# Reordering the start of an attention and mixture-of-experts kernel: later loads, q by pairs, v first

## The chip, the cores and the metric

The kernel runs on one core of a Trainium2 chip. The metric is the time of one execution in microseconds (us); lower is better. TensorE (PE) multiplies, VectorE (DVE), ScalarE (ACT) and GpSimd (POOL) do the rest, and every data transfer of this kernel is issued from one queue, that of SyncE (SP).

## The reference

The input x is 8 batches of 512 tokens of 256 numbers. Per batch (layernorm over the last axis, no scale or offset):

```
n  = layernorm(x)
q, k, v = split(n @ w_in.T + b_in)                  # 16 heads of 16
att = softmax(einsum('blhd,bmhd->blmh', q, k) / 4, axis=2)
opt = einsum('blmh,blhd->blhd', att, v)             # row sums of att, times v
x1 = x + layernorm(opt @ w_out.T + b_out)
f  = layernorm(x1)
e  = argmax(f @ gate_W.T + gate_b)                  # one of 8 experts
h  = relu(f @ wi_W.T + wi_b + (f @ lora_A[e].T) @ lora_B[e].T)
out = x1 + layernorm(h @ wo_W.T + wo_b)
```

The attention weights are summed, not multiplied with v, so what the kernel needs of each head is the maximum and the sum of the exponentials of each score row, 128 rows by 512 at a time. All is in float32. To keep precision, factors of the dense products are split into a high part and a low part (names that end in h and l), and a product is made of three.

## The kernel before, in words

**Tiling.** A batch is two *units* of 256 tokens, a unit two *chunks* of 128. The 16 heads make eight *pairs*, and pairs 0 to 3 come from the first half of the heads (group 0), 4 to 7 from the second (group 1). Per batch:

- `prepare`: x is normalised (`st_x`, `mv_x`, `nr_x`, `ln_x`, with the batch's number behind), transposed on TensorE (`pst_xn`) and split into `xnh` and `xnl` (lines 521 and 528).
- `project`: for each group, TensorE makes q and then k in `psqk` (line 486, six products of 512 columns each). For batch 0, ScalarE writes the high part and VectorE the low part of a tile `hl_0_group_t`, t being 0 for q and 1 for k (lines 362 and 375). Later batches go through `full_qk` on ScalarE and then GpSimd.
- `lay_out_k` (line 572): two transfers from SP copy a pair's k into `rows_batch_pair`. `lay_out_q`: for the first unit of batch 0 two transfers per pair (line 593) into one of three buffers, `q_0_pair`; for every other unit four transfers per pair and unit (line 606) into one of six constant tiles q0 to q5, in which the other head's half is zero.
- `scores`: a product per head and chunk (`sc`, line 642, all 128 rows; in the first unit of batch 0 two products of 64 rows, line 651), the row maximum on VectorE (`nmax`, line 661), the exponential with its sum on ScalarE (line 670). There are five score buffers.
- `values`: v of a unit, in twelve products of 256 columns (`psv`) and two ScalarE evictions (line 709).
- `attend` and `feed`: the rest of a unit, with `bout`, `gb`, `wga` and `wob` as constants, and the experts' weights `wi` and `wo` (split on GpSimd into `wih`, `wil`, `woh`, `wol`) and the low-rank weights `lb` (rounded in `lbh`, line 1166, completed in `lbs`, line 1171, which also needs the small column `low`).

**Order.** A planner (`Plan.order`) simulates the five engines with costs and due times and gives one list of operations. `settle` then moves some operations of the list by hand, with `behind(last, ops)`: it takes `ops` out and puts them just behind `last`. Each engine issues its operations in the order of the final list, and each queue, SP's too, is strictly in that order: an operation that waits holds up all behind it on its engine. Tiles share buffers, so that an operation also waits until a buffer it reuses is free; `psqk`, `psv` and the transposes share three buffers of PSUM.

**SP's order at the start, before.** x of batch 0 in two halves, two loads of wqk, bqk, wv, wout, lb, wi_0 to wi_3, x of batches 1 to 3 (`xt_1` to `xt_3`), wga_f, gb, low, bv, bout, wob; then, behind the first k (`hl_0_0_1`), q and rows of pairs 0 and 1, wo_0 to wo_3, q and rows of pair 2, rows of pair 3; then rows of pairs 4 to 7 and q of pairs 3 to 7 between those of the second unit, which the planner issues interleaved, one transfer for each of several pairs in turn.

**Other engines at the start, before.** VectorE runs `lbh` right after the last `xnl_0`, ahead of the first `hl`. TensorE makes `psqk_0_0_0`, `psqk_0_0_1`, `psqk_0_1_0`, then v of both units, then `psqk_0_1_1`. GpSimd splits wih/wil 2 and 3 right behind `nr_x_1` and ahead of `nr_x_2`, in both versions. After pair 2's scores TensorE transposes parts of batches 1 and 2 between the score pairs (`pst_xn_1_0` between pairs 2 and 3).

Of the kernel before, what the change touches and what calls it, by code (L numbers as in the profile page):

```python
# [26 lines left out]
PE, ACT, DVE, POOL, DMA = "PE", "ACT", "DVE", "POOL", "DMA"  # L27
# [155 lines left out]
def kernel(  # L183
# [72 lines left out]
    behind = [0.0]  # L256
# [235 lines left out]
    def units(b):  # L492

        return (0, 1), (2, 3)
# [689 lines left out]
    for b in range(B):  # L1184
# [6 lines left out]
        for i, cs in enumerate(apart):  # L1191
            for p in range(NPR):
                at = t + STEPS * i + p * len(cs)
# [17 lines left out]
    def settle(done):  # L1211


        def of(eng, *marks):
            return [o for mark in marks for o in done if o.eng == eng and o.mark == mark]

        def behind(last, ops):
            for o in ops:
                done.remove(o)
            i = done.index(last) + 1  # L1220
            done[i:i] = ops


        behind(of(DVE, "ln_x_0_2")[-1], of(DVE, "bqk"))
        lbh = of(DVE, "lbh_0", "lbh_512")
        behind(of(DVE, "xnl_0")[-1], lbh)
        st2, turns = of(DVE, "st_x_2"), of(DVE, "hl_0_0_0", "hl_0_0_1", "hl_0_1_0")
        st1, maxes = of(DVE, "st_x_1"), of(DVE, "nmax_0_0_1_1", "nmax_0_2_0_1")
        behind(turns[0], st1[:2])
        behind(turns[1], st1[2:] + of(DVE, "mv_x_1"))  # L1230
        behind(turns[2], st2[:2])
        behind(maxes[0], st2[2:] + of(DVE, "mv_x_2"))
        behind(of(DVE, "nmax_0_2_0_1")[0], of(DVE, "st_x_3", "mv_x_3"))
        lbs = of(DVE, "lbs")
        behind(of(DVE, "nmax_0_1_1_1")[0], lbs[:1])
        behind(of(DVE, "nmax_0_3_0_1")[0], lbs[1:])
        behind(of(DVE, "nmax_0_4_1_1")[0], of(DVE, "wga"))


        nr = [[o for o in done if o.eng == POOL and o.mark == f"nr_x_{i}"] for i in range(4)]  # L1240
        wih, wil = of(POOL, "wih"), of(POOL, "wil")
        woh, wol = of(POOL, "woh"), of(POOL, "wol")
        behind(of(DVE, "mv_x_1")[-1], nr[1] + [wih[2], wil[2], wih[3], wil[3]])
        behind(of(DVE, "mv_x_2")[-1], nr[2])
        behind(of(POOL, "ln_x_2_2")[-1], nr[3])
        behind(
            [o for o in of(POOL, "ln_x_3_0")][-1], [woh[0], wol[0], woh[1], wol[1]]
        )
        behind(of(POOL, "hl_1_0_0")[-1], [woh[2], wol[2], woh[3], wol[3]])
        calm = Op()  # L1250
        calm.eng, calm.mark = POOL, None
        calm.fn = lambda: nc.gpsimd.tensor_scalar(
            calm_sb(), state[0]["xn"]()[:, 1, :1], 1.0, 0.0, ALU.mult, ALU.add
        )
        last = of(DVE, "ln_x_0_2")[-1]
        early = [o for o in done[done.index(nr[0][-1]) + 1 : done.index(last)] if o.eng == POOL]
        behind(last, early)
        done.insert(done.index(last) + 1, calm)


        rows = []
        for p in range(NP):
            if p < X1B:
                rows += of(DMA, f"q_0_{p}")
            rows += of(DMA, f"rows_0_{p}")
            if p == 1:
                rows += of(DMA, "wo_0", "wo_1", "wo_2", "wo_3")
        behind(turns[1], rows)


        extra = of(PE, "psu")[FIRST:]
        return [o for o in done if o not in extra]

    done = settle(plan.order())

    name = f"{B - 1}_{units(B - 1)[-1][0]}"
# [3 lines left out]
    i = [k for k, o in enumerate(done) if o.mark == f"mv_z_{name}_1"][-1] + 1  # L1280
# [90 lines left out]
QB = 6  # L1371
# [69 lines left out]
```

## Time and profile before

| what | us |
|---|---|
| three runs | 514.71, 515.66, 515.97 (median 515.66) |
| profiled execution | 513.44 |
| its span, first to last instruction | 511.6 |
| first q transfer issued | 15.79 |
| first scores | 21.11 |
| first product of the second unit | 50.15 |
| TensorE at half its clock | 23.1 to 53.8, 70.8 to 77.7 |

The page lists busy time by engine, the span in 40 slices (12.8 us each), DMA queues, the chain that ended last, the costliest groups and the DMA issues. A timeline row is start, length, engine, line, operation, output<-inputs, shape, count, and in brackets the idle time before it and what ended it. A row of the waits is the waiting queue and line, whom it waited for, total us, times, longest. A row of the windows is the stretch, its length, busy us and count for TensorE, its weight loads, VectorE, ScalarE and GpSimd, then the granted TensorE clock, the DMA share and GB/s. "SPq" marks an issue by SP.

### The profile page before, as it was taken

The numbers are of one execution on the slowest core, as the hardware profiler recorded it, in microseconds if no ns is written. First come the engines' busy times: TensorE is split into PE (matmuls) and PEld (weight loads), VectorE is DVE, ScalarE is ACT, GpSimd is POOL, SyncE is SP. The second block draws the span as 40 slices with busy tenths as digits, with TensorE's granted clock in tenths as the row PEclk, the third lists the DMA queues.
The fourth block names the chain that finished last, engine by engine and source line by source line (L and its number), as shares of the span: only waits on it lengthen the run. The fifth ranks groups of instructions, "written<-read, shape, count | busy, mean of one in ns | idle before, by whom it ended". The sixth has DMA issues, their size and how long they took to land.

```text
span 511.6 us, 11203 instructions
## 1 busy us (share of the span) xinstructions
PE 483.8 (95%) x3134; PEld 423.7 (83%) x3134; DVE 467.3 (91%) x1056; ACT 436.4 (85%) x1205; POOL 390.1 (76%) x615
## 2 busy tenths in 40 slices
PE   7769989999999999999999999999999999998995
PEld 6534837879888988989989988989899988998995
DVE  6788999999999999999999999999999999998633
ACT  3569999998999999998999899999999989995210
POOL 7867455565889987997979998696878767888652
PEclk9955879999999999999999999999999999999999
DMA  8772263334423443244423442244224432200001
GB/s 273 217 196 68 52 154 71 89 69 112 111 51 106 113 111 68 69 121 104 105 50 120 101 102 75 51 113 110 66 70 94 114 87 67 48 26 2 21 22 42
DMA packets 41182, 46.56 MB, mean 91 GB/s; under 512 B 11326, under 2 KB 28222, under 8 KB 41120
## 3 DMA queue, kind: packets, MB, share of 16 engines
q1 hardware_dynamic: 41120, 45.84, 35.2%
q8 instruction: 26, 0.43, 0.3%
q14 instruction: 36, 0.29, 0.2%
HBM read 8.05 MB, written 4.19 MB: 24 GB/s over the span
## 4 chain that ended last, share of the span: by engine, by line
PE 62%; DVE 24%; ACT 4%; DMA 3%; issue 2%; SPq 2%; POOL 1%; POOLq 0%; ACTq 0%; DVEq 0%
PE sc L642 16%; PE psz L486 14%; DVE nmax L661 13%; PE psh L486 12%; PE psqk L486 7%; PE psy L486 3%; ACT sc L670 3%; PE psv L486 3%; PE psh L960 2%; DVE st_x L399 2%; PE sc L651 1%; DMA q<-hl 1%; DMA rows<-hl 1%; DVE hTh L300 1%; PE pst_x L469 1%
## 5 line engine op out<-in xcount | busy, mean ns | idle before, releaser
L670 ACT ACTIVATE sc<-sc,nmax 128x512 f32<-128x512 f32 x512 | 342.6, 689 | 17.1 <-DVE nmax L661 10.6
L661 DVE TENSOR_REDUCE nmax<-sc 128x1 f32<-128x512 f32 x512 | 325.4, 678 | 9.2 <-PE sc L651 4.2
L642 PE MATMUL sc<-rows,q 128*128 128x512 f32 x480 | 182.6, 423 | 5.6 <-ACT sc L670 3.1
L670 ACT ACTIVATION_READ_ACCUMULATOR sc<-sc,nmax 128x1 f32 x512 | 120.6, 236 | 0.0
L642 PEld LDWEIGHTS sc<-rows,q 128*128 128x128 f32 x480 | 88.7, 192 | 25.7 <-ACT sc L670 18.7
L486 PE MATMUL psz<-woh,hTh 128*128 128x256 f32 x256 | 73.0, 285 | 0.8 <-DVE xnl L528 0.5
L486 PE MATMUL psh<-x2h,wih 128*128 128x256 f32 x256 | 73.0, 285 | 0.0
L486 PE MATMUL psz<-woh,hTl 128*128 128x256 f32 x256 | 72.2, 282 | 0.0
L486 PE MATMUL psz<-wol,hTh 128*128 128x256 f32 x256 | 72.1, 282 | 0.0
L486 PE MATMUL psh<-x2h,wil 128*128 128x256 f32 x256 | 72.0, 281 | 0.0
L486 PE MATMUL psh<-x2l,wih 128*128 128x256 f32 x256 | 72.0, 281 | 0.0
L306 POOL TENSOR_TENSOR hTl<-full_h,hTh 128x512 fp32r<-128x512 f32 x44 | 56.9, 1294 | 2.3 <-DVE hTh L300 1.1
L486 PEld LDWEIGHTS psz<-wol,hTh 128*128 128x128 f32 x256 | 48.2, 188 | 3.6
L486 PEld LDWEIGHTS psh<-x2l,wih 128*128 128x128 f32 x256 | 48.2, 188 | 3.2
L486 PEld LDWEIGHTS psz<-woh,hTh 128*128 128x128 f32 x256 | 48.2, 188 | 2.1 <-POOL hTl L306 0.7
L486 PEld LDWEIGHTS psh<-x2h,wih 128*128 128x128 f32 x256 | 48.3, 189 | 1.1 <-DVE y L777 0.2
L486 PEld LDWEIGHTS psz<-woh,hTl 128*128 128x128 f32 x256 | 48.2, 188 | 0.2 <-POOL hTl L306 0.2
L486 PEld LDWEIGHTS psh<-x2h,wil 128*128 128x128 f32 x256 | 48.2, 188 | 0.0
L306 POOL TENSOR_TENSOR hl<-full_qk,hl 128x512 fp32r<-128x512 f32 x28 | 36.3, 1295 | 1.2
L384 ACT ACTIVATE full_h<-psh 128x512 f32<-128x512 f32 x44 | 26.4, 605 | 8.6 <-PE psh L960 8.1
L298 POOL TENSOR_SCALAR hl<-full_qk 128x512 fp32r<-128x512 f32 x28 | 17.3, 619 | 18.2 <-ACT full_qk L384 17.5
L486 PE MATMUL psqk<-xnh,wqkh 128*128 128x512 f32 x64 | 27.6, 431 | 0.7 <-ACT xnh L521 0.7
(132 smaller groups left out, 1021.4 us busy)
## 6 DMA issues: line engine op xcount, KB each, us to landing
rows<-hl SPq DMA_DIRECT2D x128, 128.0 KB, 2.6
q<-hl SPq DMA_DIRECT2D x480, 32.0 KB, 2.0
out<-ln_z SPq DMA_DIRECT2D x15, 256.0 KB, 2.2
xt<-in_x SPq DMA_DIRECT2D x7, 512.0 KB, 3.8
wi<-in_wi SPq DMA_DIRECT2D x4, 256.0 KB, 6.4
q<-hl SPq DMA_DIRECT2D x16, 64.0 KB, 2.2
wo<-in_wo SPq DMA_DIRECT2D x4, 256.0 KB, 4.5
xt<-in_x SPq DMA_DIRECT2D x2, 256.0 KB, 2.7
```

The lines of the kernel that those rows point to most:

```text
L298: nc.gpsimd.tensor_scalar(pick_hi(), pick(), 1.0, 0.0, ALU.mult, ALU.add)
L300: nc.vector.tensor_copy(pick_hi(), pick())
L306: e.tensor_tensor(pick_lo(), pick(), f32(pick_hi()), ALU.subtract)
L384: lambda: nc.scalar.activation(full(), flat(ps()), func, **kw()),
L399: DVE, 335, lambda c=c: nc.vector.bn_stats(st()[:, c, :], sel()[:, c, :]),
L469: nc.tensor.transpose(ps()[:, dc, c * P : (c + 1) * P], src()[:, c, dc * P : (dc + 1) * P], ident(),)
L486: nc.tensor.matmul(ps, w, xx, start=start and i == 0, stop=stop and i == len(terms) - 1)
L642: nc.tensor.matmul(sc(), q()[:, e, cols], k(), start=True, stop=True)
L651: nc.tensor.matmul(sc(), q()[rows, 0, cols], k()[rows], start=True, stop=True)
L661: lambda sc=sc, nmax=nmax: nc.vector.tensor_reduce(nmax(), sc(), AX.X, ALU.max, negate=True),
L670: lambda sc=sc, nmax=nmax, esum=esum, i=i, h=h: nc.scalar.activation(sc(), sc(), AF.Exp, bias=nmax(), accum_out=esum()[:, i, h : h + 1]),
L960: nc.tensor.matmul(ps()[:, i, :], lbs()[:KL, fs], axs()[:KL, : n * P], start=False, stop=i == 1,)
```

## The change

No operation is added or removed. Only `settle` differs, so only the order of the list:

- **Loads.** wi_2 and wi_3 go behind pair 1's rows, low and xt_3 behind pair 2's rows, wo_0 to wo_3 behind q of pair 6, and wga_f, gb, bout and wob behind the second unit's first two pairs of q. wi_0, wi_1, xt_1, xt_2 and bv stay in front.
- **q and rows.** The first transfer of rows_0_4 goes behind the second group's k, rows_0_7 behind q of pair 5, q of pairs 6 and 7 behind the scores of pairs 3 and 4. The second unit's first 24 q transfers keep their places in the list but are sorted, four of one pair in a row.
- **v.** On TensorE `psqk_0_1_0` now follows v's products, `psqk_0_1_1` too; on ScalarE v's evictions precede both `hl` of the second group.
- **VectorE.** bqk and the first `wqkl` go behind the first rows' `ln_x`, the second `wqkl` between the two `xnl_0`. `lbh` goes behind the first k, with `st_x_2` and `mv_x_2`. The second group's k (`hl_0_1_1`, low part) goes behind the second row maximum of all. `st_x_3` goes behind maxima of pairs 3 and 4, `wga` to the second unit (pair 2).
- **GpSimd.** `nr_x_3` goes behind `mv_x_3`, together with `ln_x_3_0`.

```diff
-        behind(of(DVE, "ln_x_0_2")[-1], of(DVE, "bqk"))
-        lbh = of(DVE, "lbh_0", "lbh_512")
-        behind(of(DVE, "xnl_0")[-1], lbh)
-        st2, turns = of(DVE, "st_x_2"), of(DVE, "hl_0_0_0", "hl_0_0_1", "hl_0_1_0")
-        st1, maxes = of(DVE, "st_x_1"), of(DVE, "nmax_0_0_1_1", "nmax_0_2_0_1")
-        behind(turns[0], st1[:2])
-        behind(turns[1], st1[2:] + of(DVE, "mv_x_1"))
-        behind(turns[2], st2[:2])
-        behind(maxes[0], st2[2:] + of(DVE, "mv_x_2"))
-        behind(of(DVE, "nmax_0_2_0_1")[0], of(DVE, "st_x_3", "mv_x_3"))
+        norms, wqkl, xnl = of(DVE, "ln_x_0_2")[-1], of(DVE, "wqkl"), of(DVE, "xnl_0")
+        behind(norms, of(DVE, "bqk") + wqkl[:1])
+        behind(xnl[0], wqkl[1:])
+        q0, k0, q1, k1 = of(DVE, "hl_0_0_0", "hl_0_0_1", "hl_0_1_0", "hl_0_1_1")
+        st = [of(DVE, f"st_x_{i}") for i in range(4)]
+        mv = [of(DVE, f"mv_x_{i}") for i in range(4)]
+        behind(q0, st[1][:2])
+        behind(k0, st[1][2:] + mv[1] + of(DVE, "lbh_0", "lbh_512") + st[2] + mv[2])
+        behind(of(DVE, "nmax_0_0_0_1")[0], [k1])
+        behind(of(DVE, "nmax_0_3_1_1")[0], st[3][:2])
+        behind(of(DVE, "nmax_0_4_0_1")[0], st[3][2:] + mv[3])
...
-        behind(of(DVE, "nmax_0_4_1_1")[0], of(DVE, "wga"))
+        behind(of(DVE, "nmax_0_2_3_1")[0], of(DVE, "wga"))
+        v = [[o for o in done if o.eng == eng and (o.mark or "").startswith(name)]
+             for eng, name in ((PE, "psv_0"), (ACT, "v_0"))]
+        behind(v[0][-1], of(PE, "psqk_0_1_0"))
+        behind(v[1][-1], of(PE, "psqk_0_1_1") + of(ACT, "hl_0_1_0", "hl_0_1_1"))
+        behind(of(ACT, "hl_0_1_0")[-1], [q1])
...
-        behind(of(DVE, "mv_x_2")[-1], nr[2])
-        behind(of(POOL, "ln_x_2_2")[-1], nr[3])
+        behind(mv[2][-1], nr[2])
+        behind(mv[3][-1], nr[3] + of(POOL, "ln_x_3_0"))
...
-            if p == 1:
-                rows += of(DMA, "wo_0", "wo_1", "wo_2", "wo_3")
-        behind(turns[1], rows)
+            rows += of(DMA, *({1: ["wi_2", "wi_3"], 2: ["low", "xt_3"]}.get(p, [])))
+        behind(k0, rows)
+        behind(k1, of(DMA, "rows_0_4")[:1])
+        q5, q6, q7 = (of(DMA, f"q_0_{p}") for p in (5, 6, 7))
+        behind(q5[-1], of(DMA, "rows_0_7"))
+        behind(of(PE, "sc_0_3_1_0")[-1], q6 + of(DMA, "wo_0", "wo_1", "wo_2", "wo_3"))
+        behind(of(PE, "sc_0_4_1_0")[-1], q7)
+        names = [f"q{i}" for i in range(QB)]
+        at = [i for i, o in enumerate(done) if o.eng == DMA and o.mark in names][: 4 * QB]
+        pairs = sorted((done[i] for i in at), key=lambda o: o.n)
+        for i, o in zip(at, pairs):
+            done[i] = o
+        behind(pairs[7], of(DMA, "wga_f", "gb", "bout", "wob"))
```

## The prediction

> **What bounds the kernel now.** I read the page first (busy shares, slices, chain), then for the first 95 us the timelines of SP, TensorE, VectorE and GpSimd, the waits of SP's queue, and the windows of clock.
>
> ```profile
> PE 483.8 (95%) x3134; PEld 423.7 (83%) x3134; DVE 467.3 (91%) x1056; ACT 436.4 (85%) x1205; POOL 390.1 (76%) x615
> PEclk9955879999999999999999999999999999999999
> ```
>
> From slice 6 (about 77 us) TensorE is busy at full clock to the end, so whatever time the front saves or loses should arrive at the end. The change touches only the front. Of the SP queue's timeline (start, length, count):
>
> ```profile
> 14.45 0.33 SPq L284 DMA_DIRECT2D wob<-in_wob  x1
> 15.79 1.97 SPq L593 DMA_DIRECT2D q<-hl  x2
> 17.85 1.19 SPq L572 DMA_DIRECT2D rows<-hl  x2
> 19.10 1.25 SPq L593 DMA_DIRECT2D q<-hl  x2
> 20.39 1.24 SPq L572 DMA_DIRECT2D rows<-hl  x2
> 21.67 2.01 SPq L284 DMA_DIRECT2D wo<-in_wo  x4
> ...
> 43.86 21.92 SPq L606 DMA_DIRECT2D q<-hl  x34
> 65.88 9.60 SPq L572 DMA_DIRECT2D rows<-hl  x14
> 75.52 3.14 SPq L606 DMA_DIRECT2D q<-hl  x5
> 78.76 1.21 SPq L572 DMA_DIRECT2D rows<-hl  x2
> 80.01 4.41 SPq L606 DMA_DIRECT2D q<-hl  x7
> ```
>
> The reader is to see that this queue never rests: 34 issues in 21.92 us are 0.645 us each, and from 15.79 to 83.84 us there are 103 steps in 68.05 us. SP is an engine without a busy row on the page, yet it is full until past 84 us. Its waits in this stretch are few:
>
> ```profile
> SPq L593 <- DMA xt<-in_x: 1.6, 2, 0.9
> SPq L284 <- DMA lb<-in_lb: 1.5, 1, 1.5
> ```
>
> The first two q issues wait for bulk loads of x (landed 15.71 and 17.14 us) that they don't read: each issue up to there starts just as the one eight places before it has landed. So the loads ahead hold back the first q. VectorE and TensorE:
>
> ```profile
> 11.02 2.97 DVE L1166 CAST lbh<-lb 98x512 fp32r<-98x512 f32 x2
> 13.91 0.74 DVE L375 SCALAR_TENSOR_TENSOR hl<-psqk,bqk,hl 128x512 fp32r<-128x512 f32 x1
> ```
>
> ```profile
> 29.55 1.22 PE L651 MATMUL sc<-rows,q 64*128 64x512 f32 x4 [4.22 <-DMA rows<-hl]
> 30.71 1.11 PE L469 MATMUL pst_xn<-ident,ln_x 128*128 128x128 f32 x4
> 85.92 1.09 PE L642 MATMUL sc<-rows,q 128*128 128x512 f32 x4
> ```
>
> VectorE sits in lbh before the first hl. The third pair's scores wait 4.22 us for rows queued behind wo. And the scores at 85.92 us (batch 1, first unit, pair 2): the last q transfer they need is the issue at 83.84 us, landed after 2.0 us, at 85.8; by the times in between, the half that reads it ran at about 86.2. SP is only 0.35 us ahead there. The next pair has 3.0 us, earlier ones 2 to 15.
>
> **Startup edits.** Moving one wqkl behind ln_x and one between the xnl keeps VectorE's sum before the second product (four ln_x, bqk, two wqkl, two xnl), which started at 7.16 and can start at 7.08: under 0.1 us, taken as 0. With lbh behind k, the low half of q starts when ScalarE's high half is done, 13.3 instead of 13.91, and ends at 14.0; k ends at 15.4. Without eight loads in front (wi_2, wi_3, xt_3, wga_f, gb, low, bout, wob; bv stays), q issues at 14.05 instead of 15.79 (-1.74); the second no longer waits. Two q and two rows issues at 0.64 put the second pair's q at 16.70 instead of 19.10: **-2.40 on SP**.
>
> TensorE still has 24 psv and 24 psqk products ahead of the first scores in whichever order, ending near 19.6 as before; v ahead of the second group of heads costs and brings nothing there, since the PSUM buffers it takes are free (k's low half at 15.4, v's eviction near 17.6). First scores 19.6 instead of 21.1: -1.5. If v's eviction came late, psqk_0_1_1 would start late by the same amount. The last hl now stands between the second and third row maximum: 0.65 us of VectorE, a 0.6 us hole in ScalarE, closed because pair 1's rows land only near 21.3.
>
> **Third and fourth pair.** Two wi loads (1.0 us) replace four wo (2.05) ahead of pair 2, whose rows land near 25 instead of 29.4. But a wait is added on GpSimd: wih[2] waits for wi_2, issued at 19.3; the four wo took 3.7 to 5.1 us from issue to landing, so it is there at 23.0 to 24.4. Queued behind it are wih/wil 2 and 3 (3.9 us), nr_x_2 (1.45) and ln_x_1 (1.3): 29.6 to 31.0. pst_xn_1_0 waits for that, ahead of pair 3's scores on TensorE, and xnh_1 stands ahead of pair 2's last exponentials on ScalarE. So against 30.71 now this place gains 1.1 at best and may lose 0.3. low is issued after pair 2's rows, lands near 25 and is asked for by lbs near 25.6: 0, or up to 0.5 us of VectorE.
>
> From there TensorE runs at half clock to the second unit. Its own work from 30.71 to 50.15 is about 18 us of 19.4, the rest waits for ScalarE that go when the maxima aren't split by st_x_3 (1.76 us, moved 5 us later): -1.1 to -2.8 at the second unit, I take -2.3. wga (0.75) moves from 41.6 into the second unit, where VectorE is full: -1.7. Grouping the second unit's q by pairs costs nothing: the same 24 issues, and each pair is complete 2 us or more before its scores. q_0_6 and q_0_7 land 3 and 1 us ahead of theirs. **Compute would arrive at 85.92 about 1.7 us early (0 to 2.8).**
>
> **The queue takes it back.** The eight loads are now issues inside the full stretch: wi 2 x 0.48, xt 0.62, low 0.38, wga_f, bout, wob 0.38 each, gb 0.43 (their lengths before plus the 0.05 us step) = 3.5 us; wo only changes place. Another 0.2 us goes where rows_0_4 waits for VectorE now. At the issue of 83.84: -2.40 - 0.20 + 3.53 = **+0.9 us**. Bounds: 0.64 each, like q, gives +2.5; 0.33 each, like the small loads alone, and one 0.4 us hole at 47 gone, gives -0.4. I take +0.9 because the same transfers show their own lengths. The last half of that q lands at 86.7, its score runs at 86.8 instead of 86.2: TensorE +0.5 (bounds -0.75 to +2.1, the gain capped by SP's place less 0.35). Until then the engines wait for 2 us; after it the order is unchanged, and SP is ahead again near 109 us, where it waits 0.5 us for buffers.
>
> Sum for the profiled execution: 513.44 (span 511.6) + 0.5 = 513.9. That execution is 2.2 under the median of the runs, 515.66, so the median after is 516.2. A difference under 0.3%, 1.55 us, counts as none.
>
> On loading, the Trainium skill speaks against the change: "DMA: Bandwidth & Descriptors", Rules for kernel authors, says to issue a DMA early and wait late. By that rule the eight loads would stay in front, SP's place at 83.84 would not move and the time would be 515.66; by the rows it is 516.2.
>
> **Rivals.** *Slower: the pause halves TensorE's clock.* If compute comes about 2 us early and SP late, TensorE idles some 2 to 2.5 us near 85.
>
> ```profile
> 67.50:70.00 2.50, 1.82 (x5) 0.74 (x4) 2.50 (x7) 2.50 (x10) 1.16 (x2) 1.00 0.75 190
> 70.00:72.50 2.50, 1.70 (x4) 0.68 (x3) 2.50 (x7) 2.24 (x7) 0.76 (x2) 0.67 0.71 169
> 80.00:82.50 2.50, 1.53 (x12) 1.47 (x12) 2.42 (x5) 2.50 (x8) 2.34 (x3) 1.00 0.57 130
> ```
>
> Five 512-column products in 2.5 us (0.23 us each at full clock, under half the time) and the clock column falls; twelve mixed ones and it holds. The stretch lasted 6.8 us. One half of that, 3.4 us at half speed where TensorE is full, costs 1.7: 513.44 + 0.5 + 1.7 = 515.6, a median of 517.9. It decides once the pause passes about 2 us; for it: the fall at 70.9; against it: the hole near 81, which left the clock alone. The skill's "TensorE: Matmul & The Clock Gate", Part 1, has the clock fall after a wholly idle window of about 3.4 us; by it this pause is too short and the price 0, but the fall above came with products still running. At SP's upper bound alone the time is 515.66 + 2.1 = 517.8.
>
> *Faster: SP does not hold the scores.* If the loads cost SP little and the compute gain passes whole, 515.66 - 1.7 = 514.0, and 512.9 with -2.8. For it: three stalls in the front go (lbh, the first q, the third pair); against it: 103 steps without a rest. It needs SP at -1.4 or earlier, outside my bounds.
>
> *The front gains nothing*, because GpSimd waits for wi: SP is still the later one, 516.2, or 515.7 if SP is on time.
>
> **How the numbers follow.** Queue takes it back (with the last rival): 0.44. Slower by clock or by dear issues: 0.36. Faster: 0.20. The first case's own range is 514.9 to 517.2. The whole range, 513.6 to 518.2, leaves out the deep end of the gain and clock loss on top of dear issues. Chances: faster 0.20, within 0.3% 0.44, slower 0.36.
>
> **What would show it.** First q issue near 14.05; first scores near 19.6; pair 2's near 25; a GpSimd wait for wi until 23 to 24.4 and pst_xn_1_0 at 29.6 to 31; the second unit near 48; SP at the named q near 84.7, with TensorE waiting for q just before 86.8 and ScalarE and VectorE idle beside it. If SP passes that issue before 82.5, or the scores there run before 85 us, the forecast is wrong on the fast side; a half-clock stretch after 84 us makes it wrong on the slow side.

## The result: slower by 0.6%, where no change was forecast

After takes 519.15 us by the median of 20 executions (516.06 to 523.41), before 516.05 (514.43 to 519.65) beside it: a ratio of 1.0059, 95% interval 1.0035 to 1.0084. The profiled execution took 516.85 us (span 515.1), that of before 513.44. The forecast was 516.2 with a range to 518.2, so the result lies beyond its slow end. Three executions in the runs below took far longer than the others of their kernel (1152.90 us of before, beside E1 to E4; 912.41 of E4, the one that was profiled; 529.18 of E17), and the ratios leave them out.

The page after, busy line and clock slices:

```profile
PE 484.3 (94%) x3134; PEld 422.9 (82%) x3134; DVE 466.7 (91%) x1056; ACT 437.8 (85%) x1205; POOL 390.8 (76%) x615
...
PEclk9855979999999999999999999999999999999999
```

TensorE is busy 0.5 us longer than before and ScalarE 1.4, VectorE 0.6 less; TensorE spends the rest of the 3.4 us idle. SP's timeline after (start, length, engine and line, output<-input, count):

```profile
13.99 1.33 SPq L593 DMA_DIRECT2D q<-hl  x2
15.90 1.19 SPq L572 DMA_DIRECT2D rows<-hl  x2
17.14 1.23 SPq L593 DMA_DIRECT2D q<-hl  x2
18.41 1.24 SPq L572 DMA_DIRECT2D rows<-hl  x2
19.70 1.08 SPq L284 DMA_DIRECT2D wi<-in_wi  x2
...
23.33 0.58 SPq L284 DMA_DIRECT2D low<-in_low  x1
23.95 0.51 SPq L269 DMA_DIRECT2D xt<-in_x  x1
...
45.62 0.58 SPq L284 DMA_DIRECT2D wga_f<-in_wga  x1
46.24 0.44 SPq L284 DMA_DIRECT2D gb<-in_gb  x1
46.74 0.42 SPq L284 DMA_DIRECT2D bout<-in_bout  x1
47.20 0.43 SPq L284 DMA_DIRECT2D wob<-in_wob  x1
47.67 20.67 SPq L606 DMA_DIRECT2D q<-hl  x32
68.44 9.50 SPq L572 DMA_DIRECT2D rows<-hl  x14
```

The first q leaves 1.80 us earlier than before, the second pair's 1.96 earlier; the rows of batch 1 leave 2.56 later (68.44 against 65.88). Between, the queue has taken on the eight loads. The last q of pair 2 (batch 1, first unit) is issued at 86.29 us instead of 83.84 and lands at 88.25. The waits of q for loads of x have gone from SP's list; the first q now waits for its own data:

```profile
SPq L593 <- DVE hl L375: 5.0, 1, 5.0
```

VectorE's timeline shows why: the first low part no longer stands behind `lbh`.

```profile
13.22 0.75 DVE L375 SCALAR_TENSOR_TENSOR hl<-psqk,bqk,hl 128x512 fp32r<-128x512 f32 x1 [2.25 <-ACT hl L362]
...
16.73 0.98 DVE L1166 CAST lbh<-lb 98x512 fp32r<-98x512 f32 x1
```

GpSimd's waits in the front (engine and line, awaited, total, times, longest) and TensorE's timeline after:

```profile
POOL wih L298 <- DMA wi<-in_wi: 4.4, 1, 4.4
```

```profile
25.77 1.29 PE L651 MATMUL sc<-rows,q 64*128 64x512 f32 x4 [1.38 <-ACT sc L670]
29.90 1.45 PE L469 MATMUL pst_xn<-ident,ln_x 128*128 128x128 f32 x4 [2.84 <-POOL ln_x L450]
...
88.34 0.94 PE L642 MATMUL sc<-rows,q 128*128 128x512 f32 x3 [2.64 <-issue]
94.17 0.47 PE L642 MATMUL sc<-rows,q 128*128 128x512 f32 x1 [1.18 <-ACT xnh L521]
```

Two rows are places where a late q holds TensorE: 88.34 starts 0.09 us behind the landing at 88.25, and 94.17 just behind that of pair 4's last q at 94.08. The releasers named in the brackets (issue, xnh) don't fit; the landings do. The windows of the first (length, then PE, PEld, DVE, ACT, POOL busy, clock, DMA, GB/s):

```profile
82.50:85.00 2.50, 2.50 (x18) 2.32 (x17) 2.36 (x10) 2.50 (x9) 1.54 (x2) 1.00 0.55 128
85.00:87.50 2.50, 0.71 (x4) 0.23 (x2) 1.03 (x3) 2.10 (x6) 1.72 (x5) 1.00 0.23 52
87.50:90.00 2.50, 1.66 (x11) 1.55 (x12) 1.15 (x2) 0.36 (x1) 1.02 (x1) 1.00 0.23 53
```

TensorE runs almost dry from 85 to 87.5 us (0.71 us busy), ScalarE behind it from 87.5 to 90 (0.36), and the clock column stays at 1.00 in this execution.

Followed along the row maxima (`nmax`), after stands against before at -1.45 us at the first, -0.64 from 62 us to 82.5 us, +1.90 at pair 2's second head half, +2.67 from pair 4 on, +3.41 at 157 us, and +3.3 at the end. So the front was ahead, and three places gave it back with interest. Two of them are the late q of pairs 2 and 4 (+2.5 and +0.77). The third, +0.60 of the +0.74 up to 157 us, is not the queue's: a cast of h on VectorE took twice its time. From the timelines of before, after and E2 (before's order but for one unit's q, described below):

```profile
156.28 0.59 DVE L300 CAST hTh<-full_h 128x512 fp32r<-128x512 f32 x1
159.08 1.20 DVE L300 CAST hTh<-full_h 128x512 fp32r<-128x512 f32 x1
156.85 1.17 DVE L300 CAST hTh<-full_h 128x512 fp32r<-128x512 f32 x1
```

Every profile in which this cast took 1.17 to 1.20 us steps by about 0.6 us there, E2's with before's loads too; none in which it took 0.62 or less does. What makes it long is not shown. That profile of before is of its fastest execution; its other ones are looked at below.

### The profile page after: what moved, and what is told of

It reads as the page before. It is cut to its first block, busy times and chain, and to the rows that moved or that the text cites. A ratio compares the mean times of both kernels' runs of the same rounds, so it can differ in the third digit from the quotient of the medians.

```text
span 515.1 us, 11207 instructions
## 1 busy us (share of the span) xinstructions
PE 484.3 (94%) x3134; PEld 422.9 (82%) x3134; DVE 466.7 (91%) x1056; ACT 437.8 (85%) x1205; POOL 390.8 (76%) x615
## 4 chain that ended last, share of the span: by engine, by line
PE 61%; DVE 22%; ACT 6%; issue 3%; POOL 1%; DMA 0%; SPq 0%; POOLq 0%; ACTq 0%; DVEq 0%
PE sc L642 15%; PE psz L486 14%; DVE nmax L661 14%; PE psh L486 12%; PE psqk L486 6%; ACT sc L670 4%; PE psy L486 3%; PE psv L486 2%; PE psh L960 2%; DVE st_x L399 1%; PE psg L811 1%; PE sc L651 1%; PE pst_x L469 1%; PE psg L814 1%; PE pst_o L469 1%
## 5 line engine op out<-in xcount | busy, mean ns | idle before, releaser
L642 PEld LDWEIGHTS sc<-rows,q 128*128 128x128 f32 x480 | 89.0, 192 | 29.6 <-ACT sc L670 21.4
```

Of the source, the lines that this page charges most:

```text
L642: nc.tensor.matmul(sc(), q()[:, e, cols], k(), start=True, stop=True)
```

## Experiments

Times are compared with executions of before on the same chip. "Half-clock time" is span x 2 x (1 - mean granted clock). Offsets are those of the row maxima against before's first profile.

| kernel | median us | ratio to before | 95% interval |
|---|---|---|---|
| after | 519.15 | 1.0059 | 1.0035 to 1.0084 |
| E1 after, one unit's q by pairs | 520.40 | 1.0063 | 1.0029 to 1.0098 |
| E2 before, the same | 517.57 | 1.0015 | 0.9991 to 1.0038 |
| E3 after, four loads in front | 517.54 | 1.0010 | 0.9981 to 1.0040 |
| E4 before, eight extra loads | 526.56 | 1.0181 | 1.0142 to 1.0220 |
| E5 E1 with xt_4 earlier | 517.78 | 1.0020 | 0.9989 to 1.0051 |
| E6 E5, four loads in front, wga's old place | 515.48 | 0.9985 | 0.9961 to 1.0009 |
| E7 after, all eight loads in front | 516.72 | 0.9993 | 0.9969 to 1.0017 |
| E9 after, all units' q by pairs, xt_4 earlier | 515.70 | 0.9977 | 0.9951 to 1.0002 |
| E10 E9 with all eight loads in front | 512.79 | 0.9937 | 0.9914 to 0.9961 |
| E11 E9, four loads in front, wga's old place | 513.24 | 0.9942 | 0.9917 to 0.9967 |
| E12 before, all units' q by pairs, xt_4 earlier | 514.44 | 0.9967 | 0.9947 to 0.9988 |
| E14 E9 with wi_2, wi_3 in front | 514.57 | 0.9943 | 0.9917 to 0.9969 |
| E15 E14 with xt_5 earlier | 515.00 | 0.9979 | 0.9949 to 1.0008 |
| E16 E15 with xt_6 earlier | 512.00 | 0.9903 | 0.9865 to 0.9940 |
| E17 E10 with xt_5, xt_6 earlier | 512.58 | 0.9910 | 0.9879 to 0.9940 |

The theory to test: the eight loads, moved into a queue that never rests, make q late, and what waits for q sets the end. Rivals: the clock (longer pauses bring half-clock stretches), and the front (the reordered second unit, or GpSimd's wait for wi).

### E1 and E2: one unit's q a pair at a time

```diff
+        names = [f"q{i}" for i in range(QB)]
+        qs = [o for o in done if o.eng == DMA and o.mark in names]
+        ns = {o.n for o in sorted(qs, key=lambda o: o.n)[40:64]}
+        at = [i for i, o in enumerate(done) if o.eng == DMA and o.n in ns]
+        pairs = sorted((done[i] for i in at), key=lambda o: o.n)
+        for i, o in zip(at, pairs):
+            done[i] = o
```

> The kernel after, with the q transfers of pairs 2 to 7 of batch 1's first unit issued a pair at a time in the same 24 places of the SP queue (before, pair 2's four transfers are spread over 8.3 us). Queue theory (the loss is SP's place at the last q of pair 2): that transfer is issued near 79.9 us instead of 86.3, the scores of pair 2 no longer wait for it, the front's gain of about 0.6 us passes, and the end is 0.6 us ahead of before: about 512.8 us for a profiled execution, a median near 515.4, 3 us or more under after. Clock theory (more half-clock windows in part of the executions, caused in the front): little changes, a median near 519 with a spread of 7 us. Front theory (the reordered second unit or GpSimd's wait costs it): median near 519, the scores of pair 2 late by 2 us although their q is there.

> The kernel before with the same pair-at-a-time order of batch 1's first unit, nothing else. Queue theory: there the last q of pair 2 was 0.35 us ahead of its scores, so nothing is won: 513.4 profiled, a median within 0.3 us of before's. If this gains 1 us or more, the q order has a worth of its own and the comparison of e1 with before must be read against this kernel.

E1's time was missed by 5 us: 520.40, as slow as after. The place itself did what the queue theory said: the last q of pair 2 landed at 82.24, four microseconds early, and nothing waited for it. Pair 2's second maximum stood at +0.40 instead of +1.90 (and not at -0.6, since the half-clock stretch near 70 us lasted 10.24 us there, 6.83 in after). But the next transfer in the late queue took over. E1's timelines of TensorE and VectorE:

```profile
86.32 1.09 PE L642 MATMUL sc<-rows,q 128*128 128x512 f32 x4
...
106.37 0.72 PE L469 MATMUL pst_x<-ident,ln_x 128*128 128x128 f32 x4 [2.28 <-DVE hTl L369]
```

```profile
103.37 1.41 DVE L399 BATCH_NORM_STATS2 st_x<-xt 128x6 f32<-128x256 f32 x4 [1.20 <-DMA xt<-in_x]
```

VectorE waited 1.20 us for `xt_4` (x of batch 4, issued at 99.81 in the same queue), `hTl` behind it came late, TensorE paused 2.28 us, and its clock was halved from 106.77 for 3.41 us: the offset went from +0.40 to +3.15. (Of the rest of its lateness, 1.3 us come at 420 us; more on that place under E18.) E2 shows no gain from this sorting alone (1.0015, interval across 1; its median was 0.9 us over before's, where 0.3 at most was expected).

### E3 and E4: fewer and more loads in the stretch

```diff
-        behind(pairs[7], of(DMA, "wga_f", "gb", "bout", "wob"))
+        behind(of(DMA, "xt_2")[-1], of(DMA, "wga_f", "gb", "bout", "wob"))
```

> The kernel after with four of the eight moved loads (wga_f, gb, bout, wob) back in front of the first q. Queue theory: the four took 2.05 us of SP between 45.6 and 47.7 us; without them the last q of pair 2 is issued at 84.2 and lands at 86.2, its score runs near 86.3 and the end is about 2 to 2.5 us ahead of after, within 0.3 us of before: a median near 515.9. The first q stays near 14.0, since the issue eight places before it lands before that. Clock theory or front theory: no change against after, near 519.

E3 fell to a ratio of 1.0010: nearly the whole loss went. At an equal half-clock time of 38 us (a line through each kernel's executions, 0.42 to 0.45 us per us) it stands at 515.4, before at 515.4, after at 517.0. The last q of pair 2 was issued at 85.51 and not 84.2, in an execution whose front was slower, and pair 2's scores were not held; pair 4's still were:

```profile
93.35 0.47 PE L642 MATMUL sc<-rows,q 128*128 128x512 f32 x1 [1.14 <-ACT xnh L521]
```

E4 adds eight loads of gb to before, behind the second unit's last q, into tiles that nobody reads:

```diff
+        for t in spare:
+            o = Op()
+            o.eng, o.mark, o.n = DMA, "spare", 0
+            o.fn = lambda t=t: nc.sync.dma_start(out=t(), in_=gb.partition_broadcast(P))
+            behind_q = [x for x in done if x.eng == DMA and getattr(x, "n", 0) == 445][0]
+            done.insert(done.index(behind_q) + 1, o)
```

> The kernel before with eight extra loads of gb into tiles that nobody reads, on SP behind the last q of pair 7 of the second unit (60 us). Queue theory: 0.58 + 7 x 0.48 us on SP, about 4.0; the last q of pair 2 (batch 1) lands at 89.8 instead of 85.8, its maximum moves from 86.96 to 90.4, and the whole rest of the kernel with it: +3.4 us, a median near 519.4. If the queue does not hold the scores: 0. If the longer pause near 88 us brings TensorE's clock down as well: 1.7 to 3.4 us more, 521 to 523, in part of the executions or all, with a half-clock stretch after 86 us.

The direction is the queue theory's, the size is not: 1.81% or some 9 us instead of 3.4, with 51.6 us of half-clock time against 41.1. E13 is the same kernel again, for its profile:

> The kernel before with eight extra loads once more, for its profile. Queue theory alone: the maximum of pair 2's second head half (batch 1) moves from 86.96 to about 90.4, and the end by 3.4 us. Its five timed runs were 9 us over before, at 10.5 us more half-clock time. Clock theory for the rest: half-clock stretches of 3.4 us or more after 86 us, which the kernel before does not have there, and two or more later gates (xt_4 near 104 us, pair 2 of batch 2) where the engines wait for SP again.

The eight took 0.43 to 0.58 us each to issue (60.85 to 64.76), but landed 1.2 us apart. Each of the next issues started just behind the landing of the one eight before it (67.36 behind 67.34, 68.65 behind 68.59, 69.84 behind 69.82), so five of these q's waited 0.46 to 0.75 us more each. The last q of pair 2 was issued at 90.54, 6.7 us late. E13's timeline of TensorE (one line of code is added above, so line 642 is 643):

```profile
92.60 1.62 PE L643 MATMUL sc<-rows,q 128*128 128x512 f32 x3 [3.19 <-DMA q<-hl]
```

It waits 3.19 us for q; a half-clock stretch of 3.41 us begins at 92.18, and the one at 71.70 lasts 10.24 us instead of 6.83. The offset at that score is +6.45, behind it +7.7. The queue and the clock both act; that the queue's pause set off the stretch at 92.18 is the likely reading, of one profile.

### E8 and E18: both kernels again

> The kernel after once more, for a second profile of it. Clock theory for the spread: the times of after run from 516.1 to 523.4 with mean clocks of 0.963 down to 0.950, 0.42 us for each us at half clock. A profile at a lower clock should show extra stretches of 3.4 us at half clock beside the two that the first profile has (22.6 to 53.3, 70.3 to 77.2), each worth about 1.4 us; if it lies at full clock after 77 us and is late by another way, this falls. Queue theory for the gate: the scores of pair 2 wait for the q issued near 86.3 again.

519.48 us at a mean clock of 0.957. The named q was issued at 87.40 and landed at 89.36:

```profile
89.45 0.94 PE L642 MATMUL sc<-rows,q 128*128 128x512 f32 x3 [1.81 <-ACT sc L670]
```

The windows of the same execution:

```profile
87.50:90.00 2.50, 0.69 (x4) 0.49 (x4) 0.74 (x2) 1.53 (x4) 2.17 (x5) 1.00 0.22 50
90.00:92.50 2.50, 2.50 (x14) 2.45 (x12) 1.84 (x3) 1.45 (x4) 0.47 (x1) 0.56 0.23 52
```

Behind the same wait the clock falls at 90.31 for 3.41 us; the offset goes from +2.99 to +4.79. So in part of after's executions the pause also costs a half-clock stretch, which the first profile does not show. Over after's 20 executions 43.4 us were at half clock, over 24 of before 41.1: at 0.42 us each the difference is 1.0 us of the 3.

> The kernel before once more, for a second profile. If the queue holds before as well in part of its executions: TensorE waits for q or VectorE for xt somewhere between 84 and 230 us, 1 us or more, and the time is 515 to 519. If not, those waits stay under 0.5 us as in the first profile, and a longer time comes from half-clock stretches alone.

518.75 us. Nothing waits between 84 and 230 us, so the expectation's place was wrong; but later in its timeline TensorE waits for q in before too, in the last batch:

```profile
420.24 1.10 PE L642 MATMUL sc<-rows,q 128*128 128x512 f32 x2 [1.57 <-DMA q<-hl]
```

A half-clock stretch follows at 420.34. In before's first profile the same wait was 0.34 us, so the offsets behind 418 us are against an execution that was spared. In the profiles here of kernels whose last batch has interleaved q (E4's execution of 912 us aside), TensorE waits there for a q each time: 0.68 us in after's first (its score at 421.06 follows a landing at 420.92), and 1.47 to 2.31 in E1 to E3, E5 to E8, E13 and here; in E9 to E12 and E14 to E17, whose q is sorted in every unit, it doesn't.

### E5 to E7: the second place, and the loads put back

E5 adds to E1 one line; E7 drops the two lines that move the eight loads from after.

```diff
+        behind([o for o in done if o.eng == DMA and o.n == 843][0], of(DMA, "xt_4"))
```

> The kernel after, with the pair-at-a-time order of batch 1's first unit and xt_4 (x of batch 4) issued six places earlier, near 96.5 us instead of 99.8. In the run with the pairs alone VectorE waited 1.20 us at 102.2 for xt_4: a second place that the late queue holds. Queue theory: with both places clear, compute's own gain of about 0.6 us passes, no TensorE wait for q at 88 and no VectorE wait for xt at 102, and at an equal amount of half-clock time (span x 2 x (1 - mean clock)) this kernel is 0.3 to 0.9 us under before, where after is 1.7 over. Clock theory: the median still lies 2 us or more over before, because the half-clock time stays 2 us or more over before's. If neither: a further gate behind 105 us shows in the profile.

Both places went: the offset was -0.25 at pair 2 and -0.26 at pair 4, against +1.90 and +2.67 in after. The gain still did not reach the end. The next unit with interleaved q (batch 2, pair 2) held TensorE, which with what follows put the offset at +0.9, and the late q of the last batch (1.70 us, half clock from 419.66) then took it from +0.96 to +3.55. The first place:

```profile
141.96 0.47 PE L642 MATMUL sc<-rows,q 128*128 128x512 f32 x1 [1.19 <-DMA q<-hl]
```

> The kernel after with all eight loads back in front; every other edit stays. Queue theory: the first q is at 15.8 again, SP passes the last q of pair 2 near 83.8 as before, its scores run near 86.3; the end is that of before, 0 to 0.6 us under it at equal half-clock time, and 1.5 to 2.3 under after: the moved loads are the loss, the other edits are worth 0 to 0.6. If the other edits (v, lbh, st_x, wga, second unit's order) are the loss: it stays 1.5 over before.

With the loads alone undone, after's other edits bring the time of before (0.9993). Compute was 1.9 us ahead at 82.5 us, more than in after; the last q of pair 2 was issued at 84.89, 1.05 us later than in before, where the same place was expected, and took it back:

```profile
28.67 1.11 PE L469 MATMUL pst_xn<-ident,ln_x 128*128 128x128 f32 x4
...
86.95 0.93 PE L642 MATMUL sc<-rows,q 128*128 128x512 f32 x3 [2.54 <-ACT sc L670]
```

The first of these lines tells the other half: without a wait of GpSimd for wi, `pst_xn_1_0` starts at 28.67 us although the first q left 1.9 us later than in after, where it starts at 29.90.

E6 adds to E5 the four loads in front and wga's old place:

> The same with wga_f, gb, bout and wob back in front of the first q, and VectorE's cast of wga back in the first unit (before the change's place, near 40 us). Queue theory: SP is 2 us earlier in the whole stretch and the 0.65 us that the cast costs in the second unit goes: 1.0 to 1.5 us under before at an equal amount of half-clock time, median near 515. It is the candidate for a version that beats both. If the front's gain doesn't pass at all: equal to before.

0.9985 with an interval across 1: not shown to be faster. Its profile, of an execution of 519.48 us, waits 2.31 us for the last batch's q at 421.07 and has a half-clock stretch there.

### E9 to E12: q by pairs in every unit

```diff
+        names = [f"q{i}" for i in range(QB)]
+        at = [i for i, o in enumerate(done) if o.eng == DMA and o.mark in names]
+        pairs = sorted((done[i] for i in at), key=lambda o: o.n)
+        for i, o in zip(at, pairs):
+            done[i] = o
+        behind([o for o in done if o.eng == DMA and o.n == 827][0], of(DMA, "xt_4"))
```

> The kernel after, with q issued a pair at a time in every unit of every batch (the same places of the queue, sorted) and xt_4 five places earlier. With the pairs in one unit alone the next interleaved unit (batch 2, pair 2) became the gate: TensorE waited 1.2 us for q there. Queue theory: no TensorE wait for q over 0.3 us is left up to 165 us, the front's 0.6 us reaches the end: mean and median 0.3 to 1.0 us under before, 3 us under after. If gates are not the loss: 517 to 519.

> The same on the kernel with all eight loads back in front of the first q. There compute stood 1.9 us ahead of before at the scores of batch 1's pair 1, and lost 2.4 us of it at pair 2 to the last q, which landed at 86.86. Queue theory: the 1.9 us pass: 1.5 to 2.0 us under before (about 515.0 by the mean). If the 1.9 us came from the place of the clock's windows in that one execution: 0 to 0.7 under before.

> The kernel after with wga_f, gb, bout, wob in front, the cast of wga in its old place, q a pair at a time in every unit and xt_4 earlier. Against the run with the pairs in one unit (515.5, ratio 0.9985 to before): 0 to 0.7 us better, as the later gates go too: ratio 0.997 to 0.9985.

> The kernel before with q a pair at a time in every unit and xt_4 five places earlier: what the sorting is worth alone. Queue theory: in before each gate had 0.35 to 1 us of slack, so 0 to 0.3 us: ratio 0.9995 to 1.0005. If it is 0.997 or less, the gains of the three kernels beside it are the sorting's, not the front's.

E9 turned after's 1.0059 into 0.9977 with the loads still late. No wait for q was left up to 157 us. But part of this gain before has too: E12, before with the same sorting, came to 0.9967, and against it E9 is 1.26 us slower by the medians, where after was 3.10 slower than before. So some 60% of the loss was a matter of when q and xt_4 come. E10 and E11 did better than expected: E10 took 3.75 us less than before by the medians instead of 1.5 to 2.0 (its profile stands at -1.6 from pair 1 of batch 1 on). E12 is a miss: sorting with the earlier xt_4 is worth 0.33% alone, not 0 to 0.05%. By the mark set before it ran (0.997 or less) the gains of the three kernels beside it are the sorting's; of E10's 3.75 us 2.10 are E12's too, and 1.65 are left. E18 names what before loses, the late q at 420 us and in some executions the half clock behind it; E12's profile has neither. That this is all of the 0.33% is not shown. By the ratios late loads still cost 0.4% with q sorted (E9 against E10, whose intervals overlap a little). E9's timelines show two places for it, on TensorE and on VectorE:

```profile
29.65 1.44 PE L469 MATMUL pst_xn<-ident,ln_x 128*128 128x128 f32 x4 [2.75 <-POOL ln_x L450]
```

```profile
165.99 1.41 DVE L399 BATCH_NORM_STATS2 st_x<-xt 128x6 f32<-128x256 f32 x4 [2.61 <-DMA xt<-in_x]
```

In E10 the first starts at 28.17, and the wait for xt_5 is 0.28 us.

### E14 to E17: wi in front, and the loads of x

E14 takes wi_2 and wi_3 out of E9's queue, back in front:

```diff
-            rows += of(DMA, *({1: ["wi_2", "wi_3"], 2: ["low", "xt_3"]}.get(p, [])))
+            rows += of(DMA, *({2: ["low", "xt_3"]}.get(p, [])))
```

> The kernel with q a pair at a time in every unit and xt_4 earlier (late loads), with wi_2 and wi_3 alone back in front. If GpSimd's wait for wi ate the front's gain: pst_xn_1_0 moves from 29.65 to 28.2 to 28.7, compute is 1.0 to 1.5 us further ahead at 79 us, and the mean falls from 515.5 to 514.0 to 514.5. If the difference to the kernel with all loads in front lies in the later queue: 515.5, no change, with pst_xn_1_0 early all the same.

`pst_xn_1_0` started at 26.84 us (29.65 in E9), and compute was 3.1 us ahead of before from 62 to 157 us (E9: 1.2 at 62 us). GpSimd's wait for wi had eaten 2 us of the front. Then, at 160 us, 3.8 us went at one place. VectorE's timeline, E14, and that of E15, where xt_5 is issued at 154.72 instead of 159.74:

```profile
163.69 1.41 DVE L399 BATCH_NORM_STATS2 st_x<-xt 128x6 f32<-128x256 f32 x4 [3.67 <-DMA xt<-in_x]
```

```profile
221.82 1.08 DVE L399 BATCH_NORM_STATS2 st_x<-xt 128x6 f32<-128x256 f32 x3 [3.25 <-DMA xt<-in_x]
```

> The kernel with wi_2 and wi_3 in front, q a pair at a time and xt_4 earlier, and now xt_5 (x of batch 5) six places earlier as well, near 155.5 us instead of 159.7. Queue theory: VectorE no longer waits for xt_5 at 160 us (3.67 us there), the 3.1 us that compute is ahead of before at 157 us reach the end: 2 to 3.5 us under the run without this edit, which has a mean of 514.7, so 511 to 512.5; ratio to before 0.990 to 0.992. If the wait only stood for another that ends just behind it: 514 to 514.7.

E15's time was missed: the 2.7 us passed 160 us, and were lost at 222 us to xt_6. E16 moves that too, E17 does both on E10:

```diff
+        behind([o for o in done if o.eng == DMA and o.n == 1361][0], of(DMA, "xt_5"))
+        behind([o for o in done if o.eng == DMA and o.n == 1879][0], of(DMA, "xt_6"))
```

> The kernel with wi_2 and wi_3 in front, pairs, xt_4 and xt_5 earlier, and now xt_6 (x of batch 6) four places earlier, near 213 us instead of 217. Queue theory: no VectorE wait for xt at 222, the 2.7 us ahead of before pass 165, 222 and stay to the end but for single half-clock stretches: mean 512 to 513, ratio 0.990 to 0.993. If the gain is taken back again: 514.5 to 515.5, and the profile names the place.

> The kernel with all eight loads in front, pairs and xt_4 earlier (512.8 median, ratio 0.9937, no wait for xt over 0.3 us), with xt_5 and xt_6 earlier too. Queue theory: it was 1.5 to 2 us ahead of before and met its xt loads in time, so 0 to 0.4 us: ratio 0.993 to 0.994.

E16 has the lowest ratio, 0.9903, from six executions, and E17's interval holds it. By the releasers that the view names, TensorE and VectorE wait for DMAs 0.4 us in all behind 80 us. The rows of its waits for a DMA from there on are

```profile
POOL hl L298 <- DMA q<-hl: 1.6, 2, 1.3
...
DVE st_x L399 <- DMA xt<-in_x: 0.4, 1, 0.4
```

Its profile is not the clean case that was expected: the offset is -2.4 us at 87 us, and a pause with a half-clock stretch at 103.16 took 2 us of it (the wait of 0.4 us for xt_4, at 99.77, stands just ahead of it). E17 did better than the 0.993 to 0.994 expected, 0.9910, though xt_7 held VectorE in its profile, by 1.9 us.

## Why the prediction was wrong

**Right: the mechanism and the front's numbers.** The first q (14.05 forecast, 13.99), the first scores (19.6, 19.41), pair 2's (25, 25.77), GpSimd's wait until 23.53 (23.0 to 24.4) and `pst_xn_1_0` (29.6 to 31, 29.90) all came so. SP did take the gain back, at the scores that were named, with the engines idle beside it.

**Wrong: the term +0.9 for SP's place.** It was +2.45. The eight loads were priced at 3.53 us by their lengths in the front; inside the full stretch they took 4.34 with their steps (wi 1.12, low 0.62, xt 0.55, the last four 2.05), 0.54 each: +0.8. (Their lengths in the front come to 3.33, as wi_2 and wi_3 took 0.33 there, not 0.43.) The gain at the start was 1.96, not 2.40, since the first rows waited for k until 15.90: +0.4. The rest came to +0.07 where a gain of 0.20 was forecast: +0.3, waits of single issues, among them two of 0.2 us for wo's landings. The upper bound, +2.5, came this near by chance: it priced each load like a neighbouring q, at 0.64, which is too dear, and left the other two misses out. The price lay between a load's own length in the front and its neighbours' step. E7 limits this account: with the eight loads in front the same issue was still 1.05 late, so the other edits hold the queue as well. With +2.45 and the same working, 0.35 of slack away, the named score would have been forecast 2.1 late and the time 517.8, as the rival had it.

**Wrong: nothing lost behind that gate ("after it the order is unchanged, and SP is ahead again").** The working ended at one gate. SP does wait for buffers again, at the rows of 111.83 us (109.16 in before), but until then it stays 2.45 to 2.47 us late, and pair 4's last q (+0.77) came in between. (The +0.60 at 157 us is VectorE's cast, which no term foresaw.) E1 shows why one gate was not the thing to count: with it cleared, xt_4 took its place; E5, E14 and E15 add pair 2 of batch 2, xt_5 and xt_6. Each time one consumer is freed of the late queue, the next one collects.

**Wrong, without effect: compute early by 1.7.** It was 0.64. The second unit started 1.29 us early instead of 2.3, the moved `wga` cost 0.65 there, about as forecast. The place of the wait for wi gained 0.81 us (29.90 against 30.71), within the forecast; E14 shows that without the wait compute would have been about 2 us further ahead. Since SP was later still, it changed nothing in after.

**The rival of the clock** was half right. One price of 1.7 for all executions was wrong, and so was its condition, a pause past about 2 us (2.64 in after's first profile left the clock alone), but E8 shows the half-clock stretch behind the named wait, worth 1.8, in an execution of after. Over all executions the longer half-clock time is worth 1.0 of the 3 us.

**The page that spoke against the change was right here.** "DMA: Bandwidth & Descriptors", Rules for kernel authors, of the Trainium skill says to issue early and wait late. E7 and E14 agree: late loads cost compute through wi, and with them in front the same edits are worth more (0.9937 in E10 against 0.9977 in E9).

## What to carry over

A queue that issues without a rest is a resource like an engine: price a transfer that is moved into it by its length in a full queue (0.54 us here, where the front showed 0.42), and follow the lateness to every consumer behind it, not only to the first. Issue the transfers of one consumer together and in the order in which consumers need them; here this brought before 0.33%, where the change without its late loads brought nothing (E7). Where the clock's stretches move from one execution to the next, take several profiles before a wait is called harmless: before's first showed 0.34 us at 418 us, its second 1.57.

## Of the hardware, not expected

**The clock's stretches come in steps of 3.41 us** (3.41, 6.83, 10.24, 13.65, 23.89, 27.31, 30.72), and their edges differ from one execution to the next (23.05 in before, 24.39 in its second profile; 22.56 and 11.80 in after). After took 516 to 523 us, 0.42 us more for each us at half clock by a line through its executions. (The last stretch is cut by the end of the span.) Pauses of TensorE of 1.57 us (before, 420 us), 1.81 (E8), 2.28 (E1) and 3.19 (E13) met half clock (a stretch began within the pause or at most 0.9 us behind it), those of 2.64 (after) and 2.54 (E7) did not. At one place, the last batch's q near 420 us, pauses of 1.57 (E18), 1.60 (E3), 1.70 (E5) and 2.31 (E6) met it, those of 1.47 (E7), 1.53 (E8), 1.68 (E1), 1.86 (E13) and 2.02 (E2) did not, so the length of the pause alone does not decide. The Trainium skill's "TensorE: Matmul & The Clock Gate", Part 1, has the same window of about 3.4 us, free-running, so that its place varies by run; its wholly idle window is not needed by these rows, as the pauses of 1.6 to 2.3 us show.

**Small broadcast loads land slowly one behind the other**: E13's eight loads of gb were issued 0.48 us apart and landed 1.2 us apart, and held up the q's behind them, each of which started just behind the landing of the transfer issued eight places before it.
